# Mixing matrices in turn with the last unit's other side work, and three loads on GpSimd eight steps ahead

## The chip, the cores and the metric

The kernel runs on one core of one Trainium2 chip. The metric is the device time of one execution in microseconds (us), the median of three runs. A matmul runs on TensorE (PE; PEld is its load of weights), elementwise work on VectorE (DVE), exponentials and casts on ScalarE (ACT). GpSimd (POOL) and SyncE (SP) mostly issue DMAs. Each engine executes its own list of instructions in order; an engine that issues a DMA waits at that point until the semaphores for the transfer are met.

## The reference

The input `x` is (2, 128, 64, 64): two images, 128 channels, 4096 positions each.

```python
# layer 0
xn  = group_norm(x, 32 groups)
q, k, v = conv1x1(xn);  q, k = rotary2d(q), rotary2d(k)      # 4 heads of 32 channels
x   = xn + conv1x1(softmax(q k^T / sqrt(32)) v)
# layer 1, on tokens t (2, 4096, 128)
t = t + softmax(u u^T) u                    with u = layer_norm(t)
t = t + sum_i w_i * stu_i(layer_norm(t)[:, :4096 / 2**i])    # i = 0..3
w = one_hot(argmax(s)) - s + s,             s = softmax(log_weights + gumbel)
# stu(u): causal FFT convolution of u with 16 filters phi, then for each filter k
#   U_plus_k  @ M_phi_plus[i, k] * sigma_k**0.25 + U_minus_k @ M_phi_minus[i, k] * sigma_k**0.25
#   + three taps: sum_n shift(u, n) @ M_u[i, n]
```

The four branches differ only in their matrices and in where the input is cut off. So the kernel first forms one set of weighted matrices: for each filter k one plus and one minus matrix summed over the four branches (the "mixing matrices"), three tap matrices (`mu`), and a mask over the ends. That work reads only parameters and has no place of its own: it is side work, put beside the attention.

## The kernel before

The kernel has a main path in half precision (`in_halves`), which the profile shows, and a fallback that is not executed here.

*Layer 0* (`layer0`) runs four units (image b, two heads each). A unit has 16 rounds: two heads times eight chunks i of 512 queries. A round goes through 32 key tiles in 11 groups m: TensorE makes the scores of up to three key tiles (L209, called from the loop), ScalarE takes the exponential (L465), and TensorE weighs the values with it two groups later. The sum of a round lies in one PSUM accumulator `acc` with a single buffer. At the round's end `close` copies it to `accs` on VectorE (L413), and the next round's first weighing waits for that copy. Every second round `divide` (VectorE L366, L370, L371, L377, and small SP transfers) divides by the softmax sums and `project` multiplies with the output weights.

Side work is a Python generator: the loop calls `next(beside)` at certain groups of each round, and each call emits the instructions up to the next `yield`. Groups in `BESIDE` do so in the first three units, groups in `BESIDE_LAST` in the last one; other groups, in `DONE`, take a step of `divide` and `project`. In the last unit the side work is `beside_last`, 71 steps in 80 slots, one kind after another:

- nine steps of layer-norm statistics, then 17 steps of `normalise(0)`, which normalises the first image's tokens, transposes them on TensorE and splits them into the halves `hiT`, `loT`;
- `filters16`, 12 steps: loads of `phi` and `turned`, the branch weights, the 64 coefficients `coef`, eight table matmuls, and the writing of the tables to memory;
- `matrices16`, 33 steps through `combined`: for each of 16 filters, two 256 KB loads into one of two raw buffers in the tile `room` (L918, L919 on the queue `aside`, which is GpSimd), a weighted sum over the branches on VectorE (L750, L752), a sum and a difference (L929, L930), a store `mx[k]` (L931, GpSimd), and a maximum (L933).

The order of one engine's list is not always the order in the program. A scheduler places the instructions by its own estimates, except those marked `keep_in_program_order`, which include the products of layer 0 and the normalising steps. Tiles with the same `tag` share buffers and so wait for each other.

*Layer 1's attention* (`attend16`), image 0 first, goes over 36 pairs (j, i), i at least j, of blocks of 512 tokens. For a pair: `scores` makes y in two halves (L1185, three matmuls a tile), exponential on ScalarE (L1194), cast into the first part of `pair` (ScalarE, L1198), the remainder into its second part (VectorE, L1199). `turn` transposes both parts by DMA on SP (L1204) into `eT` if i > j. One pair later `direct` weighs tokens with `pair` (`od`, L1213) and adds into `oT` (L1225, L1227); two pairs later `across` adds up `eT` (`both`, L1232) and weighs with it (`oa`, L1213). `close` ends a row j.

This attention also takes side work: `chain(left, stats.steps(), rest16(p), normalise(1, ...))`, where `left` is what is left of layer 0's last division, `stats` are the second image's statistics, and `rest16` has two steps. The first, `mask_of`, loads `ends` (256 KB, L1025, GpSimd) and forms `mask`. The second, `means`, loads `mu_raw` (768 KB, L1030, ScalarE) and `gw` (128 KB, L1032, GpSimd; the matrix of the inverse transform) and forms `mu` and `gw`. Each load is emitted directly ahead of its use.

Somewhat before that GpSimd issues `fw` (L975, the matrix of the forward transform). SP also carries the first loads for the feed-forward part: two 1 MB loads `tables_a` (`chunk16`, L1483), which have buffers of their own and are placed early by the scheduler, between the transposes of `turn`.

After attention of both images come the transform of the tokens (`feed`), the convolution and mixing (L1541 to L1564), and the inverse transform (`back`).

Of the kernel before, what the change touches and what calls it, by code (L numbers as in the profile page):

```python
# [29 lines left out]
HALF = L // 2  # L30
GT = 3
BESIDE, DONE = (1, 5, 9), (2, 4, 7, 8)
BESIDE_LAST = (1, 3, 5, 6, 9)
NJ = HALF // P
NG = 32
NK = 16
# [40 lines left out]
def conv_attn_hybrid(ctx: ExitStack, tc: tile.TileContext, io):  # L77
# [680 lines left out]
    def layers(st, layer0, in_halves):  # L758
# [25 lines left out]
        def normalise(b, stats, stage, gate=None):  # L784


            for i in range(NQ):
                while gate is not None and gate[0] <= i:
                    yield
                cols = bass.ts(i, 512)  # L790
                y = stage(i, 0)
                for t in range(4):
                    stats.normed(y[:, bass.ts(t, P)], 4 * i + t)
                nc.vector.tensor_copy(hi[0][:, cols], y)
                yield
                pt = side[0](f"yT{b}_{i}")
                for t in range(4):
                    nc.tensor.transpose(pt[:, bass.ts(t, P)], y[:, bass.ts(t, P)], ident)
                nc.vector.tensor_copy(hiT[0][:, cols], pt)
                staged = b == 0 and not in_halves  # L800
                low = (stage(i, 1), stage(i, 0)) if staged else (loT[0][:, cols], lo[0][:, cols])
                for n, (src, first) in enumerate(((pt, hiT[0][:, cols]), (y, hi[0][:, cols]))):
                    nc.vector.tensor_tensor(low[n], src, first, ALU.subtract)
                    if staged:
                        nc.sync.dma_start(lows[i, n], low[n])
                yield
            if in_halves:
                nc.vector.reduce_max(spread[:, 2 * NK + b : 2 * NK + b + 1], stats.rs, axis=AX.X)
                yield

        def filters16(spare):

            phi = spare.tile([P, 2, TROW], F32, tag="tab", name="phi16")
            aside.dma_start(phi, io["phi"])
# [15 lines left out]
                nc.vector.tensor_copy(kept, x)  # L830
                chosen.append(kept)
            chosen.append(coefficients(new, wbr, M_SCALE))
            yield
            both = spare.tile([P, 2, L], F16, tag="ks", name="spectra")
            for s in range(2):
                tb = both[:, s, : 4 * 2 * TROW].rearrange("w (h i x) -> w h i x", h=2, i=2)
# [112 lines left out]
        def beside_last(stage, spare=None):  # L949
            first_parts()  # L950
            stages = [stage(n) for n in range(1 if in_halves else 2)]
            stats = LayerStats(last, tok[0], "a0")
            yield from stats.steps()
            yield from normalise(0, stats, lambda i, n: stages[n][:, i])
            if in_halves:
                yield from filters16(spare)
                yield from matrices16(spare)


        left = layer0(tok, px, last, side, beside_last)  # L960
# [67 lines left out]
        def means(p, wbr):  # L1028
            mu_raw = p.tile([P, NBR, NU, C], F32, tag="raw", name="mu_raw")
            nc.scalar.dma_start(mu_raw, io["mu"].rearrange("i n d e -> d i n e"))  # L1030
            weighted_sum(mu, mu_raw, wbr)
            aside.dma_start(gw, io["gw16" if in_halves else "gw"])  # L1032
            if in_halves:
                nc.vector.scalar_tensor_tensor(
                    gw, gw, OUT_SCALE, mask.unsqueeze(1).to_broadcast([P, 2, P]), ALU.mult, ALU.mult
                )
            else:
                nc.vector.tensor_tensor(gw, gw, mask.unsqueeze(1).to_broadcast([P, 2, P]), ALU.mult)

        def rest16(p):  # L1040
            wbr, top = chosen[:2]
            mask_of(p, top)
            yield
            means(p, wbr)
            yield

        def matrices(p):
# [334 lines left out]
        with ExitStack() as l1:  # L1382
# [3 lines left out]
            with ExitStack() as part:  # L1386
                p = pool(part, "l1_a")
                gate = [0]

                def second_parts(n):  # L1390
                    if n < NQ and not in_halves:
                        low = p.tile([P, 2, 512], F32, tag="low", name=f"low{n}")
                        nc.sync.dma_start(low, lows[n].rearrange("n p c -> p n c"))
                        copy = nc.vector.tensor_copy(loT[0][:, bass.ts(n, 512)], low[:, 0])
                        if n == 0:
                            tc.keep_in_program_order(copy)
                        nc.vector.tensor_copy(lo[0][:, bass.ts(n, 512)], low[:, 1])

                def ready(i):
                    second_parts(i + 1)  # L1400

                second_parts(0)
                fw = transform(p1)

                def closed(j):
                    gate[0] = j + 1

                y = [None]

                def stage(i, n):  # L1410
                    y[0] = p.tile([P, 512], F32, tag="y", name=f"y1_{i}")
                    return y[0]

                stats = LayerStats(p1, tok[1], "a1")
                own = (rest16(p),) if in_halves else (filters(p, fw), matrices(p))
                steps = chain(left, stats.steps(), *own, normalise(1, stats, stage, gate))
                (attend16(0, p1, steps, closed) if in_halves else attend(0, p1, steps, closed, ready))
            right0.close()
            if in_halves:
# [443 lines left out]
```

## Time and profile before

| | |
|---|---|
| median of three runs | 2777.88 us (2777.81 to 2810.39) |
| the profiled execution | 2786.72 us |
| its span, first to last instruction | 2784.9 us |
| mean granted TensorE clock | 0.977 |
| HBM read, written | 212.53 MB, 23.33 MB |
| layer 0's last unit, from the copy L413 at 787.87 to the one at 1045.06 | 257.2 us |

The page of the profile gives each engine's busy time, then the span in 40 equal slices of 69.6 us in which each digit is a busy share in tenths, then the DMA queues, the chain of work that ended last, and the costliest groups of instructions. Times are us from the start of the span. A line such as "L1213 ... <- DVE pair L1199: 13.4, 2, 6.7" says that L1213 waited for L1199's `pair` on VectorE: in total, how often, the longest. The lists of single instructions give start, duration, engine, line, and in brackets the idle time before it and what ended that. PEclk is the clock that the throttle granted TensorE.

Busy time by stretch around the change, for all of the region that the change touches (columns: stretch, length, busy time and instructions of PE, PEld, DVE, ACT, POOL, then clock, DMA share, GB/s):

```profile
786.00:871.00 85.00, 78.06 (x369) 41.06 (x368) 74.86 (x241) 78.05 (x61) 24.14 (x32) 1.00 0.22 66
871.00:956.00 85.00, 75.67 (x325) 37.12 (x324) 30.73 (x63) 71.29 (x54) 37.17 (x51) 0.96 0.54 96
956.00:1045.00 89.00, 88.30 (x423) 47.75 (x423) 24.07 (x40) 85.76 (x65) 0.56 (x1) 1.00 0.02 7
1045.00:1160.00 115.00, 84.14 (x356) 37.02 (x355) 76.65 (x209) 50.84 (x107) 17.57 (x20) 0.85 0.71 123
```

The first three rows are the last unit of layer 0: VectorE is nearly full in the first, and nearly all of the GpSimd and DMA work lies in the first two. The last row is the start of the second layer's attention.

### The profile page before, as it was taken

To read this page: it belongs to the slowest core of one execution; us is meant where nothing else is said; L and a number is where in the kernel's file an instruction comes from. 1 tells how busy PE (TensorE), PEld (TensorE's weight loads), DVE (VectorE), ACT (ScalarE), POOL (GpSimd) and SP (SyncE) were. 2 spreads that over 40 slices of the span, in tenths; PEclk is the share of its full clock that TensorE was granted. 3 is DMA by queue.
4 is the path that set the end of the run, shared out by engine and by line. 5 is a ranking of instruction groups with operands and counts; after the bars stand their busy time and mean duration, and the time that the engine had idled before them with its cause. 6 is when DMAs were issued, how large, how long until landed. Compare 5 with 4: busy or idle time off the path is not lost.

```text
span 2784.9 us, 32561 instructions
## 1 busy us (share of the span) xinstructions
PE 2588.1 (93%) x11955; PEld 1276.1 (46%) x11955; DVE 1668.5 (60%) x2946; ACT 1841.3 (66%) x2059; POOL 432.5 (16%) x711
## 2 busy tenths in 40 slices
PE   5999999999998996999989988898789999999998
PEld 3555555555544452444434443343344445445444
DVE  5256564246267225767886567575456666666664
ACT  4999999999998894556644555454345555555553
POOL 2022121012124201100043100111111111111110
PEclk9999999999999997999999998999999999999999
DMA  4122220012014307655375654666666666655662
GB/s 144 35 65 67 65 65 20 7 50 74 22 39 94 67 5 135 115 107 105 69 144 110 126 96 91 154 174 156 149 167 165 200 192 181 179 206 179 185 188 87
DMA packets 351051, 311.92 MB, mean 112 GB/s; under 512 B 292816, under 2 KB 303200, under 8 KB 334432
## 3 DMA queue, kind: packets, MB, share of 16 engines
q1 hardware_dynamic: 295376, 231.71, 32.6%
q0 software_dynamic: 52512, 74.81, 11.2%
q10 hardware_dynamic: 2992, 3.22, 0.4%
q8 instruction: 96, 1.57, 0.2%
q14 instruction: 75, 0.61, 0.1%
HBM read 212.53 MB, written 23.33 MB: 85 GB/s over the span
## 4 chain that ended last, share of the span: by engine, by line
PE 30%; DMA 13%; DVE 7%; issue 1%; ACT 1%; POOL 0%; SPq 0%; DVEq 0%; ACTq 0%; POOLq 0%
PE m L1557 19%; PE cv L1541 6%; DMA eT<-pair 5%; DMA tables_b<-tables 3%; DVE pair L1199 3%; DMA base<-oc 2%; DVE both L1232 2%; PE ar L1312 1%; DMA had<-base 1%; DVE x L1549 1%; PE bk L1669 1%; DMA tables_a<-tables 1%; DMA rows<-uh 1%; PE od L1213 1%; PE pf L1328 0%
## 5 line engine op out<-in xcount | busy, mean ns | idle before, releaser
L465 ACT ACTIVATE e<-s 128x1536 f16<-128x1536 f32 (+1 forms) x704 | 938.4, 1427 | 52.9 <-PE s L209 48.3
L1549 DVE TENSOR_TENSOR x<-cv,x 128x1024 f16<-128x1024 f32 x512 | 602.3, 1219 | 302.9 <-ACT x L1548 302.9
L1548 ACT CAST x<-cv 128x1024 f16<-128x1024 f32 x512 | 493.7, 1017 | 404.4 <-PE cv L1541 389.5
L1557 PE MATMUL m<-x,mxr 128*128 128x512 f16 x2048 | 622.5, 381 | 0.0
L209 PE MATMUL acc<-e,v 128*97 128x512 f16 x2048 | 559.0, 380 | 16.4 <-DVE accs L413 13.7
L209 PE MATMUL s<-qs,ks 128*128 128x512 f16 x2048 | 559.7, 380 | 7.9 <-ACT e L465 4.3
L1557 PE MATMUL m<-x,mxl 128*128 128x512 f16 x1024 | 391.4, 382 | 3.3 <-DVE oh L1564 3.2
L209 PEld LDWEIGHTS <-v 128*97 128x97 bf16 x2048 | 255.4, 125 | 229.8 <-issue 28.9
L1194 ACT ACTIVATE ey<-y,nshift 128x512 f32<-128x512 f32 x288 | 196.0, 685 | 225.3 <-PE y L1185 135.9
L1557 PEld LDWEIGHTS <-mxr 128*128 128x128 f16 x2048 | 201.3, 98 | 242.8 <-issue 5.3
L209 PEld LDWEIGHTS <-ks 128*128 128x128 f16 x2048 | 201.0, 99 | 229.6 <-issue 46.8
L1478 POOL DMA_DIRECT2D tokens<-rows x252 | 152.9, 611 | 845.5 <-PE cv L1541 819.8
L1232 DVE SCALAR_TENSOR_TENSOR both<-eT 128x512 f16<-128x512 f16 x224 | 153.6, 686 | 135.2 <-DMA eT<-pair 124.5
L1213 PE MATMUL od<-pair,hi 128*128 128x512 f16 x576 | 189.6, 391 | 30.0 <-DVE oT L1225 15.1
L1185 PE MATMUL y<-bothT 128*128 128x512 f16 x864 | 206.5, 381 | 4.0 <-ACT ey L1194 3.0
L1199 DVE TENSOR_TENSOR pair<-ey,pair 128x1024 f16<-128x1024 f32 x144 | 175.4, 1218 | 16.0 <-ACT pair L1198 15.6
L413 DVE COPY accs<-acc 97x512 f32<-97x512 f32 x64 | 44.1, 689 | 227.3 <-PE acc L209 227.1
L1541 PEld LDWEIGHTS <-tokens 128*128 128x128 f16 x1024 | 100.6, 99 | 164.5 <-issue 68.1
L1213 PEld LDWEIGHTS <-hi 128*128 128x128 f16 x1024 | 102.6, 100 | 146.2 <-issue 35.1
L1198 ACT CAST pair<-ey 128x1024 f16<-128x1024 f32 x144 | 150.2, 1043 | 24.6 <-DMA eT<-pair 11.4
L1557 PEld LDWEIGHTS <-mxl 128*128 128x128 f16 x1024 | 101.0, 99 | 131.6 <-DVE oh L1564 10.0
L1213 PE MATMUL oa<-eT,hi 128*128 128x512 f16 x448 | 146.6, 389 | 14.3 <-DMA eT<-pair 14.3
(221 smaller groups left out, 2297.5 us busy)
## 6 DMA issues: line engine op xcount, KB each, us to landing
tables_a<-tables SPq DMA_DIRECT2D x64, 1024.0 KB
tables_b<-tables SPq DMA_DIRECT2D x64, 1024.0 KB
tokens<-rows POOLq DMA_DIRECT2D x252, 128.0 KB, 12.2
tab<-in_rot SPq DMA_DIRECT2D x32, 512.0 KB
ks<-term POOLq DMA_DIRECT2D x112, 64.0 KB, 2.2
qs<-term POOLq DMA_DIRECT2D x112, 64.0 KB, 2.1
accs<-back SPq DMA_DIRECT2D x32, 128.0 KB
room<-in_mpp POOLq DMA_DIRECT2D x16, 256.0 KB, 3.4
```

Source lines behind the costliest of these rows:

```text
L209: tc.keep_in_program_order(nc.tensor.matmul(*args, **kw))
L465: nc.scalar.activation(e[:, own, :], ps[:, own, :], AF.Exp, scale=SCORE_SCALE)
L1185: nc.tensor.matmul(ps[:, q, :], a[0][:, bass.ts(t, P)], c[0][:, bass.ts(i, 512)], start=(n == 0), stop=(n == 2),)
L1194: nc.scalar.activation(e[:, q, :], ps[:, q, :], AF.Exp, bias=nshift16, accum_out=den[:, t, i : i + 1])
L1199: nc.vector.tensor_tensor(pair[:, 1, own], e, pair[:, 0, own], ALU.subtract)
L1213: nc.tensor.matmul(acc, a[0][:, own], pair(m, t), start=(start and t == 0 and n == 0), stop=(stop and t == 3 and n == 2),)
L1232: nc.vector.scalar_tensor_tensor(both, eT[:, 0, :, u, :], 1.0, eT[:, 1, :, u, :], ALU.mult, ALU.add, accum_out=den[:, 4 * i + u, j : j + 1],)
L1478: (nc.gpsimd if n else nc.sync).dma_start(ut[64 * copy : 64 * copy + 64], rows16[b].rearrange("h c r w d -> (h c) r w d")[:, row : row + B ...
L1541: ordered(nc.tensor.matmul(pu[:, h, :], ut[:, at, :], tt[:, :, at, :], start=True, stop=True))
L1548: nc.scalar.copy(hi, pur)
L1549: nc.vector.tensor_tensor(lo, pur, hi, ALU.subtract)
L1557: nc.tensor.matmul(acc, m, x, start=(s == 0 and i == 0), stop=(s == 1 and i == len(products) - 1))
```

## The change

Two things are changed. In the last unit of layer 0 the mixing matrices no longer follow the tables and the normalising: after the statistics, each slot takes a step of `normalise` and `filters16` and of `matrices16` in turn (`by_turns`). For this, loads, branch weights and coefficients of `filters16` move ahead of both into `branches16`, and `BESIDE_LAST` has six slots in a round, not five.

At the start of the second layer's attention, `rest16` issues the loads of `ends`, `mu_raw` and `gw` at its beginning, all three on GpSimd and into tiles without a shared tag. Then come the statistics' eight steps, and only then `mask`, `mu` and `gw` are formed, one step each.

```diff
-BESIDE_LAST = (1, 3, 5, 6, 9)
+BESIDE_LAST = (0, 1, 3, 5, 6, 9)
...
-        def filters16(spare):
+        def by_turns(*parts):
+            parts = list(parts)
+            while parts:
+                for part in list(parts):
+                    if next(part, parts) is parts:
+                        parts.remove(part)
+                    else:
+                        yield
+
+        def branches16(spare):
 
             phi = spare.tile([P, 2, TROW], F32, tag="tab", name="phi16")
             aside.dma_start(phi, io["phi"])
...
             chosen.append(coefficients(new, wbr, M_SCALE))
-            yield
+            chosen.append((phi, turned, most))
+
+        def filters16(spare):
+            phi, turned, most = chosen[3]
             both = spare.tile([P, 2, L], F16, tag="ks", name="spectra")
...
             yield from stats.steps()
-            yield from normalise(0, stats, lambda i, n: stages[n][:, i])
+            normed = normalise(0, stats, lambda i, n: stages[n][:, i])
             if in_halves:
-                yield from filters16(spare)
-                yield from matrices16(spare)
+                branches16(spare)
+                yield from by_turns(chain(normed, filters16(spare)), matrices16(spare))
+            else:
+                yield from normed
...
-        def rest16(p):
+        def rest16(p, steps):
             wbr, top = chosen[:2]
-            mask_of(p, top)
+            ends = p.tile([P, NBR, P], F32, name="ends")
+            aside.dma_start(ends, io["ends"].partition_broadcast(P))
+            mu_raw = p.tile([P, NBR, NU, C], F32, name="mu_raw")
+            aside.dma_start(mu_raw, io["mu"].rearrange("i n d e -> d i n e"))
+            aside.dma_start(gw, io["gw16"])
+            yield from steps
+            weighted_sum(mask, ends, top)
             yield
-            means(p, wbr)
+            weighted_sum(mu, mu_raw, wbr)
+            yield
+            nc.vector.scalar_tensor_tensor(
+                gw, gw, OUT_SCALE, mask.unsqueeze(1).to_broadcast([P, 2, P]), ALU.mult, ALU.mult
+            )
             yield
...
-                own = (rest16(p),) if in_halves else (filters(p, fw), matrices(p))
-                steps = chain(left, stats.steps(), *own, normalise(1, stats, stage, gate))
+                second = normalise(1, stats, stage, gate)
+                if in_halves:
+                    steps = chain(left, rest16(p, stats.steps()), second)
+                else:
+                    steps = chain(left, stats.steps(), filters(p, fw), matrices(p), second)
```

The remaining lines of the diff touch `means` for the fallback only.

More of the change, by code (lines that the diff above doesn't have):

```diff
@@ L1031, in means @@
             weighted_sum(mu, mu_raw, wbr)
[L1032 to L1038, printed above, removed]
-        def rest16(p):
-            wbr, top = chosen[:2]
-            mask_of(p, top)
-            yield
-            means(p, wbr)
+            nc.sync.dma_start(gw, io["gw"])
+            nc.vector.tensor_tensor(gw, gw, mask.unsqueeze(1).to_broadcast([P, 2, P]), ALU.mult)
+        def rest16(p, steps):
+            wbr, top = chosen[:2]
+            ends = p.tile([P, NBR, P], F32, name="ends")
[5 more added lines that the diff above has]
+            weighted_sum(mask, ends, top)
+            yield
+            weighted_sum(mu, mu_raw, wbr)
[3 more added lines that the diff above has]
+            )
             yield
```

## The prediction

> **What bounds the kernel now.** I read the page first, then busy time by stretches of 50 and 10 us, then the waits of the stretches in which TensorE falls short, last the order of single instructions there.
>
> ```profile
> span 2784.9 us, 32561 instructions
> PE 2588.1 (93%) x11955; PEld 1276.1 (46%) x11955; DVE 1668.5 (60%) x2946; ACT 1841.3 (66%) x2059; POOL 432.5 (16%) x711
> PE   5999999999998996999989988898789999999998
> ...
> PEclk9999999999999997999999998999999999999999
> ```
>
> TensorE is the bound: 2588 of 2785 us. Only its gaps, and stretches at a low granted clock, can be won. A slice is 69.6 us. Two dents lie near the change: slice 13 (835 to 905 us, inside the last unit of layer 0) and slice 16 (1044 to 1114 us, the start of the second layer's attention, where the clock row has its only 7 of this half). Cut finer:
>
> ```profile
> 1045.80:1072.30 26.50, 11.14 (x37) 3.97 (x37) 14.34 (x29) 8.68 (x20) 6.23 (x10) 0.72 0.38 114
> 1072.30:1098.40 26.10, 26.10 (x124) 12.81 (x123) 22.88 (x61) 16.65 (x34) 2.94 (x2) 0.96 1.07 139
> 1098.40:1115.70 17.30, 6.59 (x17) 2.28 (x16) 5.51 (x29) 3.65 (x8) 2.01 (x2) 0.61 0.80 154
> ```
>
> Columns: stretch, length, busy time and instructions of PE, PEld, DVE, ACT, POOL, then clock, DMA share, GB/s. In the middle row PE fires 124 instructions in 26.1 us, about 0.21 us each: full rate. The first row has 37 (8.0 us of work in 26.5), the third 17 (3.7 us in 17.3). So 18.5 and 13.6 us are lost. The waits of PE from 1045 to 1160 name the causes:
>
> ```profile
> PE od L1213 <- DVE pair L1199: 13.4, 2, 6.7
> PE oa L1213 <- DMA eT<-pair: 13.4, 4, 9.2
> ```
>
> Who holds `pair`? The order of VectorE, ScalarE and GpSimd in the first stretch:
>
> ```profile
> 1050.71 0.35 DVE L750 TENSOR_SCALAR room<-room,small 128x256 f32<-128x256 f32 x1 [2.87 <-DMA room<-in_mpm]
> ...
> 1055.68 0.35 DVE L750 TENSOR_SCALAR room<-room,small 128x256 f32<-128x256 f32 x1 [2.08 <-DMA room<-in_mpm]
> ...
> 1058.49 1.21 DVE L1199 TENSOR_TENSOR pair<-ey,pair 128x1024 f16<-128x1024 f32 x1
> ...
> 1067.23 0.29 DVE L750 TENSOR_SCALAR mask<-ends,top 128x128 f32<-128x128 f32 x1 [6.28 <-DMA ends<-in_ends]
> ...
> 1060.56 0.39 ACTq L1030 DMA_DIRECT2D mu_raw<-in_mu  x1
> 1060.99 1.05 ACT L1198 CAST pair<-ey 128x1024 f16<-128x1024 f32 x1 [9.92 <-DVE ao L366]
> ...
> 1043.17 0.56 POOL L931 DMA_DIRECT2D mx<-room  x1 [110.27 <-DVE room L930]
> ```
>
> The last four mixing matrices stand at the very end of the unit in VectorE's order and behind it, two of them wait there for their loads, and the first `pair` comes at 1058.5. The load of the means was put into ScalarE's order ahead of a cast of `pair` and holds it until 1060.6. Then VectorE waits 6.28 us for `ends`, issued only at 1060.97, with the second half of `pair` behind it (1069.4). GpSimd stood 110 us in the store of a matrix that VectorE had not finished.
>
> **What the Trainium skill says.** "DMA: Bandwidth & Descriptors", Anatomy of one DMA: DMA engines don't wait on semaphores; the wait is on the issuing sequencer before dispatch. The trace agrees: the issue of `mu_raw` kept ScalarE idle 9.92 us. The same page, Issuing engines are not separate DMA queues: transfers of all issuers end on the same 16 engines. So putting the load on GpSimd frees ScalarE's order and gives no bandwidth. "TensorE: Matmul & The Clock Gate", What's actually happening: a TensorE that idles falls to half clock and needs some us of work to recover. Here matmuls follow at 0.43 us instead of 0.216 after the waits (1110 to 1115 us), with 0.61 granted: agrees, so a removed stall gives back more than its own length.
>
> **The change part by part.** The order of instructions of both kernels, as built, is known: on every engine it is the same again from about pair (1,2) of the first attention on. So only 786 to 1155 us can differ, and what is won or lost there shifts everything after it.
>
> *Last unit, side work.* Steps: 9 statistics, 17 normalising, 12 tables, 33 matrices, 71 of 80 slots before; now 70 of 96 (one yield gone, six slots a round), the matrices alternating with the rest. Nothing is added to TensorE (32 transposes, 8 table matmuls as before). In VectorE's order all 16 matrices now lie ahead of the copy of the eighth accumulator; before, 12 did and 4 came last. VectorE's work between one accumulator copy (L413) and the next is, by the durations of the trace (weighted sum 1.9 us, two differences 0.57, maximum 0.41, a normalised chunk about 3.6, a divide 4.0), before 12, 18, 16, 15, 17, 12, 12, 1 us and after 14, 16, 16, 12, 16, 11, 14, 9. The copies were 14.5 us apart undisturbed and 14.5, 16.1, 16.5, 18.4, 16.5, 18.7, 19.4, 17.0 measured. The work is the same and slightly evener. Waits come on top: a buffer is refilled 2.5 us after the store's issue, two load issues take 1.5, landing 3.3 more, and the next matrix some 2.9 of VectorE, so about 10.3 us for two matrices in two buffers, at most 2.9 in 15 us. One round of the new order has four, so I expect a wait of about 4.5 us there, and 1 to 2.5 us in three or four others; before it was 9.6 us in four waits. Against that, the scattered table writes (32 issues of 0.75 us) now come after all matrices, so no load queues behind them, but they still meet the divide's transfers: those cost PE 4.5 and 1.7 us before (waits at 908 and 941), and one of the two should stay. Sum: 0, from -7 to +9.
>
> *Start of the attention.* Removed from between the last copy and the second `pair` half: the four matrices with waits, the held issue on ScalarE, the wait for `ends`. What is then late: y of (0,0) begins at 1045.8 as before, first cast done at 1050.4 as before, `pair` half one on VectorE to 1051.6, L366 to 1052.9 (1.22 each), second cast by 1052.2, half two to 1054.1; od of (0,0) ends near 1055.5, and the point that lay at 1072.4 comes at about 1056.4. Gain 16. The loads of `ends`, means and inverse matrix (256, 768, 128 KB) are issued behind `fw`, which waits for TensorE, so at about 1045 on GpSimd in some 2.5 us; nothing urgent is behind them (the next there are eight small powers). At the 200 to 350 GB/s that the same loads reached at 1060 to 1066 they are gone by about 1053, hidden by the ramp; if they hold back the small divide transfers, 2 us are lost, since the divide's product stands ahead of a `pair`. Their first use stands some 40 places later in VectorE's order than before: no wait. The nine small operations on them (mask, means, inverse; 0.3 to 0.6 us each) move in between later ones, hidden by TensorE's 7.8 us a pair (36 matmuls at 0.216). ACT loses one issue of 0.39 us. Gain 16, from 12 to 18.
>
> *An effect on SP's order.* Before, both 1 MB loads of `tables_a` are issued together at 1084.3, ahead of the transposes of pair (0,3), which land at 1110: the 9.2 and 1.5 us waits and the slow clock of the third row, 13.6 us. In the new order one load stands before the transposes of (0,3) and the other before those of (0,4). The two transposes of a pair take 4.3 us (the usual piece of the chain of waits); 1084.3 to 1110 is 25.7 us with some 2.5 pairs of them (10.8), so the two loads cost about 15, one 7.5. A pair's transposes are ready about 11.4 us before they are needed and take 4.3: 7 us of slack. 12 us of delay beyond it gave the stall of 9 to 10. With the loads apart, the first delays by some 4.7 (no stall), the second by about 8.7: a stall of 1.7 and a little slow clock. Gain 9; bounds 0 (the loads still pile up) and 13.
>
> Sum on the profiled execution: 2786.7 (span 2784.9 and 1.8 around it) - 16 - 9 + 0 = 2761.7. It stands 8.8 above the median of 2777.9, where the same 25 us give 2753.
>
> **The rivals.**
> - *Front only:* the `tables_a` loads cost the same wherever they stand, since the same 2 MB pass the same engines. For it: DMA share 1.07 and 0.80 around there. Against: slack of 7 us for each pair. Gain 16: 2762.
> - *Slower:* the matrix loads become the pace of layer 0's last unit. All 16 matrices are now squeezed between accumulator copies, an accumulator has one buffer, and each load that lands late holds the copy behind it and TensorE behind that. It decides when the rounds carry on average 3.1 us more wait than now over eight rounds (25 us); with 5 us it is +40 - 25, 2793. For it: the round with four matrices, and 4.1 us from issue to landing. Against: two buffers, and rounds of 10 to 12 us of work that leave room.
> - *No effect:* the ramp at 1046 is held by something that I took for done (the divide's transfers, or the loads at 1045), and the new waits take the 16 us back: 2778.
>
> **How the numbers follow.** Both gains 0.55, front only 0.25, no effect 0.10, slower 0.10. Predicted 2753. The likeliest's own bounds are 2777.9 less 38 and less 3 in the extreme; its middle part 2740 to 2764. The range reaches to front only and toward no effect: 2739 to 2772. A measurement of this kernel tells about 2% (55 us) from no change; the whole lost time in the touched stretches is 18.5 + 13.6 + 25 in the unit (257 us from copy to copy, against 16 times 14.5), so faster by 2% would need nearly all of it: 0.03. Slower by over 2% needs 10 us more in each of eight rounds: 0.03.
>
> **What would show it.** Right: no wait of `od` for `pair` over 2 us and no idle ScalarE near the start; PE over 20 us busy in the 26 after y of (0,0), against 11.1; `oa` waiting under 4 us in all for `eT`; the last unit 257 us within 8. Wrong: PE waits for `accs` well over 13.5 us, VectorE waiting for `room` over 25 us in the unit, or the 9 us wait for `eT` still there.

## The result and the profile after

| | before | changed |
|---|---|---|
| median | 2788.08 us (20 runs, 2771.60 to 2814.15) | 2769.99 us (20 runs, 2749.75 to 2791.76) |
| ratio | | 0.9940, 95% interval 0.9918 to 0.9963 |
| span of the profiled execution | 2784.9 us | 2769.4 us |

The ratio is 16.7 us of 2788, with an interval from 10.3 to 22.9; it leaves out runs that took over 1.5% more than the fastest run of the same kernel, so it differs a little from the ratio of the medians. A gain of 25 was forecast. The median of before was 2777.88 when three runs were known and is 10 higher with 20, so the absolute 2753 was also set on a low level.

From the page of the changed kernel, the busy times and the rows of TensorE and of its clock:

```profile
PE 2588.8 (93%) x11955; PEld 1276.7 (46%) x11955; DVE 1670.4 (60%) x2946; ACT 1841.7 (67%) x2059; POOL 434.3 (16%) x712
...
PE   5999999999998898999989997998779999999998
...
PEclk9999999999999999999999998999999999999999
```

Busy times are the same as before, so no work went away. In slice 16 TensorE's digit is 8 where it was 6, and the 7 in the clock row is gone; slices 13 and 14, in the last unit, are both 8 now. Busy time by stretch says it more closely (columns as before: stretch, length, PE, PEld, DVE, ACT, POOL, clock, DMA share, GB/s). The first row begins at the first score matmul of the attention, as the 26.5 us row of before did; the second is the stretch with the 1 MB loads; the last three are the last unit.

```profile
1050.10:1076.60 26.50, 25.30 (x122) 12.25 (x122) 20.43 (x36) 19.80 (x41) 0.00 (x0) 1.00 0.72 102
1082.80:1097.80 15.00, 10.49 (x33) 3.85 (x32) 9.68 (x44) 4.88 (x10) 2.16 (x3) 0.78 1.10 153
786.00:871.00 85.00, 76.90 (x349) 39.39 (x347) 69.70 (x223) 76.21 (x60) 26.21 (x35) 0.96 0.25 74
871.00:956.00 85.00, 78.09 (x338) 39.15 (x338) 46.32 (x101) 71.94 (x55) 36.31 (x51) 0.96 0.48 91
956.00:1049.00 93.00, 89.74 (x423) 47.95 (x422) 20.20 (x29) 85.47 (x65) 5.63 (x9) 0.98 0.17 36
```

TensorE is busy 25.3 of the first 26.5 us of the attention, where it was 11.1, and the clock is 1.00. The last unit needs 93 us for the 423 matmuls after 956, where before it needed 89. TensorE's waits in the same 115 us of attention as before:

```profile
PE oa L1232 <- DMA eT<-pair: 3.6, 3, 1.7
PE od L1232 <- DVE oT L1246: 2.6, 2, 2.2
...
PE od L1232 <- DVE pair L1218: 0.2, 1, 0.2
```

The two waits of 13.4 us for `pair` and for `eT` have become 0.2 and 3.6, and a new one for `oT` is 2.6. (Line numbers after the change are about 20 higher.)

From here on two lengths tell the kernels apart better than the whole time does. Each is read from one trace of a kernel. The *unit* is the time from the first to the last accumulator copy of layer 0's last unit (787.87 to 1045.06 before). The *start* runs from that last copy to the 41st `pair` subtraction. Behind that point all kernels below have the same order of instructions, and this rest alone took from 1526 to 1566 us in 14 profiles. A *round* is the time from one accumulator copy to the next; the unit has 16.

| kernel | unit | start | sum against before | ratio of times (95%) |
|---|---|---|---|---|
| before | 257.2 | 198.9 | | |
| changed | 263.1 | 172.9 | -20.1 | 0.9940 (0.9918 to 0.9963) |
| changed_again | 259.2 | 171.3 | -25.6 | 0.9884 (0.9832 to 0.9936) |
| mu_on_gpsimd | 260.9 | 181.9 | -13.3 | 0.9946 (0.9919 to 0.9973) |
| early_loads | 255.5 | 182.8 | -17.8 | 0.9964 (0.9938 to 0.9989) |
| turns_only | 265.8 | 177.7 | -12.6 | 0.9944 (0.9915 to 0.9974) |
| five_slots | 271.9 | 173.6 | -10.6 | 0.9948 (0.9918 to 0.9978) |
| three_buffers | 262.6 | 171.7 | -21.8 | 0.9912 (0.9884 to 0.9940) |
| later_tables | 264.4 | 172.4 | -19.3 | 0.9961 (0.9938 to 0.9985) |
| both_mended | 266.1 | 172.1 | -17.9 | 0.9935 (0.9908 to 0.9962) |
| six_slots_no_turns | 245.1 | 217.6 | +6.7 | 0.9991 (0.9963 to 1.0019) |
| even_matrices | 265.9 | 177.7 | -12.5 | 0.9947 (0.9922 to 0.9971) |
| even_loads_together | 262.9 | 175.7 | -17.4 | 0.9925 (0.9895 to 0.9956) |
| even_clear | 246.8 | 177.9 | -31.4 | 0.9869 (0.9821 to 0.9917) |

Most of the ratios overlap. The starts tell more: those of before, of the runs with one half of the change and of the whole change lie apart (198.9; 177.7 to 182.8; 171.3 to 173.6 for the changed kernel and its variants with matrices in turn). Units repeat less well, as the traces of one order below show.

### The profile page after: what moved, and what is told of

Its sections match the earlier page's. It is cut to its first block, busy times and chain, and to the rows that moved or that the text cites. A ratio compares the mean times of both kernels' runs of the same rounds, so it can differ in the third digit from the quotient of the medians.

```text
span 2769.4 us, 32569 instructions
## 1 busy us (share of the span) xinstructions
PE 2588.8 (93%) x11955; PEld 1276.7 (46%) x11955; DVE 1670.4 (60%) x2946; ACT 1841.7 (67%) x2059; POOL 434.3 (16%) x712
## 4 chain that ended last, share of the span: by engine, by line
PE 52%; DMA 24%; DVE 14%; ACT 6%; issue 3%; POOL 1%; SPq 0%; DVEq 0%; ACTq 0%; POOLq 0%
PE m L1579 17%; PE acc L209 11%; PE s L209 11%; DMA eT<-pair 8%; PE cv L1563 5%; ACT e L465 5%; DMA tables_b<-tables 4%; DVE pair L1218 4%; DMA tables_a<-tables 3%; DVE both L1251 3%; DMA rows<-uh 2%; DMA base<-oc 2%; DMA had<-base 1%; PE bk L1691 1%; PE od L1232 1%
## 5 line engine op out<-in xcount | busy, mean ns | idle before, releaser
L209 PE MATMUL acc<-e,v 128*97 128x512 f16 x2048 | 560.7, 381 | 17.1 <-DVE accs L413 14.5
L1563 PEld LDWEIGHTS <-tokens 128*128 128x128 f16 x1024 | 100.1, 99 | 163.4 <-issue 65.7
L1232 PEld LDWEIGHTS <-hi 128*128 128x128 f16 x1024 | 102.0, 100 | 130.8 <-issue 19.3
L1563 PE MATMUL cv<-tables_b,tokens 128*128 128x512 f16 x512 | 135.0, 387 | 23.2 <-DMA tables_b<-tables 22.6
## 6 DMA issues: line engine op xcount, KB each, us to landing
tokens<-rows POOLq DMA_DIRECT2D x252, 128.0 KB, 12.6
```

Source lines behind the costliest of these rows:

```text
L209: tc.keep_in_program_order(nc.tensor.matmul(*args, **kw))
L1232: nc.tensor.matmul(acc, a[0][:, own], pair(m, t), start=(start and t == 0 and n == 0), stop=(stop and t == 3 and n == 2),)
L1563: ordered(nc.tensor.matmul(pu[:, h, :], ut[:, at, :], tt[:, :, at, :], start=True, stop=True))
```

## The experiments

### The start: which part of the change brings it

**mu_on_gpsimd**, the kernel before with one word changed:

```diff
-            nc.scalar.dma_start(mu_raw, io["mu"].rearrange("i n d e -> d i n e"))
+            nc.gpsimd.dma_start(mu_raw, io["mu"].rearrange("i n d e -> d i n e"))
```

> The kernel before with one word changed: the load of the means is issued by GpSimd in place of ScalarE; matrices and the place of all loads in the program stay. As built, this alone puts both halves of the first pairs ahead of the mask in VectorE's order and one tables_a load on either side of the transposes of pair (0,3). Theory A (the start is late for three reasons that add: four matrices at the end of the unit, the held cast with the mask behind it, two 1 MB loads together): the unit stays at 257 us, the first pair half still comes 13 us after the last accumulator copy, the second 2.6 us behind it where it was 11; that gives about 8, the separated loads another 9, so 17 us less than before. Rival B (the loads cost the same wherever they stand): 8 us less, with a wait of 9 us for eT still there. Rival C (the start is held by the matrices alone): no more than 3 us less.

Measured: the start is 17.0 us shorter, as theory A said. VectorE's list at the start of this run:

```profile
1061.28 0.42 DVE L933 TENSOR_REDUCE spread<-room 128x1 f32<-128x256 f32 x1
1061.61 1.21 DVE L1199 TENSOR_TENSOR pair<-ey,pair 128x1024 f16<-128x1024 f32 x1
...
1064.18 1.23 DVE L1199 TENSOR_TENSOR pair<-ey,pair 128x1024 f16<-128x1024 f32 x1
```

The first half of `pair` still stands directly behind the last matrix, 13.6 us after the copy at 1048.05, and the second follows 2.6 us later, where it was 11. TensorE waits for `pair` once, 6.9 us, and no 9 us wait for `eT` is left (2.8 the longest). The unit took 260.9 with the order of before (257.2).

**early_loads**, the second half of the change alone: `rest16` as in the changed kernel, the matrices as before.

> Only the second half of the change: the loads of ends, means and inverse matrix on GpSimd at the head of the attention's side work, the matrices as before, one kind after the other. The order of VectorE around the start and that of SP are those of the run with the one word changed. Theory A: within 3 us of that run, so about 17 us less than before, unit 257 us: it is the issue's engine that matters, not the eight steps. Rival (the distance matters too, because ends and means land too late): 5 us or more less than the one-word run.

Measured: start 182.8, 0.9 from the one-word run. The engine of the issue brings the gain. What distance is worth stays open: VectorE and SP have the same order in both runs, and in both `ends` was issued 16 to 17 us after the last copy (at 1059.21 here), behind the store of the last matrix on GpSimd. So the eight steps changed neither the issue nor the order of use here.

**turns_only**, the first half alone: `by_turns`, `branches16` and six slots, with `rest16` as before.

> Only the first half of the change: matrices in turn with normalising and tables, six slots a round; mask, means and inverse matrix as before, with the means on ScalarE. As built, both tables_a loads stay together ahead of the transposes of pair (0,3). Theory A: the unit takes 263 us as in the changed kernel, 6 more than before; the first pair half comes some 6 to 9 us earlier after the last copy, the wait for eT of 9 us stays; together 0 to 6 us less than before. Rival (the longer unit of the changed kernel was chance): unit 257, 6 to 12 us less.

Measured: the unit is 265.8, 8.6 above before, and theory A holds there. In the start it holds for one part, and the sum, 12.6 us below before, lies outside its 0 to 6. Two of TensorE's waits in this run:

```profile
PE oa L1227 <- DMA eT<-pair: 11.1, 2, 9.5
PE od L1227 <- DVE pair L1213: 0.9, 2, 0.4
```

The 9.5 us wait for `eT` stays, because both `tables_a` loads still stand together. But the start is 21 us shorter. The issue of `mu_raw` on ScalarE came at 1051.06, before the last accumulator copy, and held no cast. (The profile of before puts that issue's wait down to VectorE's L366, but here L366 of the last divide starts only at 1060.28; what the issue really waited for is not shown.) With the matrices gone from the end of the unit, the cast is free even with `mu_raw` on ScalarE. So the held cast was a consequence of the four matrices too, and the two halves of the change do not add: 17 (or 16) and 21 apart, 26 and 27.6 together.

### The unit: why it became longer

Three profiles with the order of before gave 257.2, 260.9 and 255.5, mean 257.9. Three with the matrices in turn gave 263.1, 265.8 and 259.2, mean 262.7. So one order spreads by 5 to 7 us, and the two groups overlap: by the totals alone the 4.8 us would be weak evidence. The last is the changed kernel once more, run beside the last arrangements:

> The changed kernel itself once more, for a second trace and for times beside the next two. Theory A (two rounds of the last unit are longer by construction, 19.8 and 19.3 us): unit 262 to 266 us, the start 172 to 174 us from the last copy to the 41st half of a pair; everything behind differs from run to run by some 20 us. Rival (the long rounds of the first trace were chance): unit 257 to 259.

Its unit, 259.2, lies between the two expectations, but its rounds have the same two long ones, 19.9 and 17.8 us, where the first trace has 19.8 and 19.3. The rounds of all six traces say more than the totals (us):

| order, three traces each | third round | eleventh round | rounds 1 to 8 together | rounds 9 to 16 together |
|---|---|---|---|---|
| as before | 16.2 to 16.5 | 14.8 | 135.5 to 137.0, mean 136.4 | 120.0 to 124.2, mean 121.5 |
| matrices in turn | 19.8 to 21.4 | 17.8 to 20.4 | 135.5 to 138.8, mean 137.0 | 123.7 to 127.0, mean 125.6 |

The third and the eleventh are longer in every trace. But the fourth, sixth and seventh became shorter by about as much as the third became longer, so that the first eight rounds, which hold all the matrices, cost the same as before. The 4.8 us lie almost wholly behind them, in the eleventh.

The third round in the changed kernel's trace, VectorE's list at its end:

```profile
831.56 0.34 DVE L750 TENSOR_SCALAR room<-room,small 128x256 f32<-128x256 f32 x1
831.94 0.48 DVE L752 SCALAR_TENSOR_TENSOR room<-room,small 128x256 f32<-128x256 f32 x1
836.03 0.35 DVE L750 TENSOR_SCALAR room<-room,small 128x256 f32<-128x256 f32 x1 [3.61 <-DMA room<-in_mpm]
836.30 0.68 DVE L413 COPY accs<-acc 97x512 f32<-97x512 f32 x1
```

VectorE has no other gap in this round. Just ahead of the accumulator copy stands the first operation of the next matrix, which waits 3.6 us for its load; TensorE waited 4.8 us for that copy. Over the unit VectorE waits 20.2 us for loads in nine places, 9.6 in four before.

The eleventh is the round from 954.93 to 974.20. The tables are written to memory in two bursts of 16 small writes, one for each half. GpSimd's and VectorE's lists:

```profile
952.41 5.98 POOL L872 DMA_DIRECT2D tables<-spectra  x8 [2.15 <-DMA tables<-tables]
...
963.83 0.52 POOL L877 DMA_DIRECT2D tables<-tables  x1 [5.44 <-DMA tables<-spectra]
964.35 0.59 POOL L989 DMA_DIRECT2D fw<-in_fw  x1
964.93 0.55 POOL L1052 DMA_DIRECT2D ends<-in_ends  x1
...
965.74 1.22 DVE L377 TENSOR_TENSOR ao<-ao,accs 32x1024 f32<-32x1024 f32 x1 [5.84 <-DMA accs<-back]
```

The same product in the kernel before, where the copy was at 955.33:

```profile
962.55 1.22 DVE L377 TENSOR_TENSOR ao<-ao,accs 32x1024 f32<-32x1024 f32 x1 [3.65 <-DMA accs<-back]
```

The second burst of table writes runs into a divide. The divide's last product (L377) comes 10.8 us after the copy at 954.93, where before it came 7.2 us after its copy and TensorE did not wait for it. This is the first divide of the last head: its projection `po` stands ahead of the next scores in TensorE's order. The delay came while the burst was under way: the reciprocal waited 1.4 us for its input, and from the issue of `back` to that of the next transfer it took 3.5 us (959.93 to 963.45), 1.3 before; the last transfer was as quick as before. TensorE waited 2.5 us, and matmuls then ran slowly (clock 0.84 from 964.5 to 975).

**five_slots** puts `BESIDE_LAST` back to `(1, 3, 5, 6, 9)` in the changed kernel.

> The changed kernel with five side slots in a round of the last unit, as before, in place of six: 70 steps in 80 slots. As built, no round has more than three matrices (the changed kernel has one with four), and the table matmuls come some two rounds later. Theory A (the unit is 6 us longer for a load wait in the round with four matrices, 3.4 us, and for table writes that meet a divide whose product TensorE waits for, 4.5 us): the unit takes 256 to 261 us, and the run is 2 to 7 us below the changed kernel, so 19 to 24 below before. Rival (the matrices in turn cost the unit 6 us in any arrangement): unit 263, same time as the changed kernel, 16 below before.

Measured: the unit is 271.9, nine *longer* than in the changed kernel, and both theories miss. The load waits did not go (20.6 us in all): the fourth round took 21.0 us, and TensorE waited 6.6 us for its copy. The bursts moved two rounds down and met two divides of the last head; their rounds, the eleventh and the thirteenth, took 19.4 and 21.4 us. The second of these:

```profile
994.50 5.22 POOL L872 DMA_DIRECT2D tables<-spectra  x7 [1.87 <-DMA tables<-tables]
...
998.38 0.34 DVE L371 RECIPROCAL rec<-rec 32x32 f32<-32x32 f32 x1 [2.41 <-DMA rec<-accs]
1005.77 1.22 DVE L377 TENSOR_TENSOR ao<-ao,accs 32x1024 f32<-32x1024 f32 x1 [7.04 <-DMA accs<-back]
```

**later_tables** delays the tables by empty steps (`for _ in range(2): yield` ahead of each half).

> The changed kernel with four empty steps ahead of the tables' halves (two ahead of the first, two more ahead of the second), so that the second burst of table writes is released by a matmul late in the 11th round, and starts some 12 us after the copy that begins a divide, not 11 us ahead of it. Theory A (a burst that meets a divide costs little where nothing waits, and 4.5 to 6 us where a projection stands behind the divide in TensorE's order): the 19.3 us round becomes 15, the wait of po under 1 us, the unit 258 to 260 us. Rival (the divide is late for another reason, or the burst only moves to the next divide): one round of 19 us or more stays, the unit 263 or more.

Measured: the eighth to eleventh rounds, 16.4, 17.4, 14.4 and 19.3 us in the changed kernel, became 14.4, 15.0, 15.0 and 15.6. That the eleventh is short again once the burst starts after its divide shows that the burst had made it long. But the thirteenth went from 15.0 to 25.0: the rival's second case. What met the divide at 981.91 was not the burst but what follows it on GpSimd:

```profile
984.97 0.52 POOL L881 DMA_DIRECT2D tables<-tables  x1 [4.95 <-DMA tables<-spectra]
985.48 0.59 POOL L993 DMA_DIRECT2D fw<-in_fw  x1
986.06 0.55 POOL L1056 DMA_DIRECT2D ends<-in_ends  x1
986.60 1.05 POOL L1058 DMA_DIRECT2D mu_raw<-in_mu  x1
987.64 0.55 POOL L1059 DMA_DIRECT2D gw<-in_gw  x1
...
997.08 1.22 DVE L377 TENSOR_TENSOR ao<-ao,accs 32x1024 f32<-32x1024 f32 x1 [11.60 <-DMA accs<-back]
```

A copy of 992 KB and loads of 256, 256, 768 and 128 KB were issued in 3.2 us, in the middle of the divide. Its 4 KB transfer `back` was issued at 985.50 and followed by the next at 991.29: 5.8 us where the kernel before had 2.1. So the early loads of the change belong to the traffic that can hurt.

**three_buffers** gives the matrices a third raw buffer.

> The changed kernel with three raw buffers for the matrices in place of two (the third takes the room of the sums, which move to the small tile). As built, the scheduler puts 1, 2, 4, 3, 4, 2 matrices into the rounds of the first half where the changed kernel has 1, 2, 3, 2, 3, 3, 2. Theory A (VectorE's waits for loads, 20 us in nine waits in the changed kernel, set the longer rounds): these waits fall under 8 us and the unit takes 258 to 260 us instead of 263 to 266. Rival (VectorE is full in these rounds, and the waits only fill what is left): the unit stays at 263 or more, with TensorE's waits for accs still 14 us or above.

Measured: VectorE's load waits fell from 20.2 to 8.8 us and the third round from 19.8 to 16.3. But two rounds then have four matrices, one of them rose to 20.9, and the unit stayed at 262.6. The rival holds: in the first seven rounds of the changed kernel VectorE's work and its waits for loads fill 114 of 120.5 us (95.6 and 18.5), and what a load wait gives back is taken by other work. TensorE's waits for `accs` add up to 15 us, as the rival said.

**both_mended** joins the two:

> The changed kernel with three raw buffers and with the second half of the tables later. If both theories hold, the unit takes 254 to 257 us, the start stays as in the changed kernel (173 us from the last copy to the 41st half of a pair, before: 199), and the run is 6 to 9 us below the changed kernel, 22 to 26 below before. If the matrices in turn cost the same in any arrangement, the unit stays at 263.

Measured: unit 266.1, with the long sixth round of one parent (20.7 us) and the long thirteenth of the other (24.7). Nothing was mended.

**six_slots_no_turns** has six slots and the early loads, with the matrices after the tables:

> The kernel before with the loads of the second half of the change and six slots in a round, but matrices still after the tables, not in turn. As built, ten of the 16 matrices stand in VectorE's order in the last round and behind it. Theory A (what stands at the unit's end in VectorE's order delays the first pairs, at about 5 us a matrix with two buffers): the middle of the unit is quick, the first pair half comes 35 to 50 us after the last copy instead of 13, and the run takes 10 to 30 us more than before. Rival (the engine is idle enough there to catch up): within 5 us of the run with only the early loads.

Measured: the unit took 245.1, the shortest of all, and the start 217.6. The first `pair` came 49 us after the last copy, as theory A said, and TensorE waited 40.0 us for it. The time of the whole is that of before, not 10 to 30 us more, since the short unit pays for most of the late start; the sum of the two stages is 24.6 us above that of early_loads, so the rival misses. In this run GpSimd's list shows where the matrices had been:

```profile
1012.48 0.56 POOL L931 DMA_DIRECT2D mx<-room  x1 [103.72 <-DVE room L930]
```

GpSimd stood 104 us in the store of a matrix that VectorE had not summed, though from 908 to 1008 VectorE was busy for 24.2 us of 100: the scheduler had put the sum behind later work in VectorE's list. The first eight rounds, here with two matrices in place of 12 or 16, take 122.5 us, 137.0 before and 136.8 in the changed kernel. That points at the matrices among the normalising, though the bursts of table writes meet other rounds here too.

### A version from these findings

**even_matrices** takes normalising and tables first, then the matrices at two a round in the second half, with their sums and what stands around them held to the program's order (`pinned` is `keep_in_program_order` under a condition; the first part is shown against the kernel before):

```diff
+                for _ in range(7):
+                    yield
-                yield from matrices16(spare)
+                for n, _ in enumerate(matrices16(spare)):
+                    yield
+                    if n % 2 == 0:
+                        yield
...
-                nc.vector.tensor_copy(accs[:, bass.ts(half, 512)], acc[: NV * CH + 1, :])
+                pinned(nc.vector.tensor_copy(accs[:, bass.ts(half, 512)], acc[: NV * CH + 1, :]), (b, h) == (B - 1, NH - 1))
```

> A new arrangement from what the runs showed: normalising and tables first, seven empty steps, then the matrices at two a round in the second half of the unit, where VectorE is idle for three quarters; their sums, the accumulator copies, the divides and the projections of the last head, mask and means are held to the program's order on VectorE, so that the scheduler can't gather the matrices at the end. The early loads of the change are kept; one tables_a load stands on either side of the transposes of pair (0,3). If the unit was long because matrices and normalising share the full rounds, the unit takes 245 to 250 us (six slots without turns: 245 without matrices in it), the start 172 to 176, so 30 to 38 us less than before and 12 to 20 less than the changed kernel. Rival (matrix loads of 10 us for two take the rounds of the second half, 14.7 us long): rounds of 16 to 18 us there, unit 260 or more.

Measured: the first eight rounds are 14.4 to 16.2 us, but three later ones 21.4 to 21.8, and the unit is 265.9. The rival's 260 or more came, but its rounds of 16 to 18 us did not. In each of the three, a matrix that stood between the divide's first sum and its second delayed the reciprocal: `back` was issued 6.5 us after the copy (942.17 to 948.70 in the first), against 3.6 for an undisturbed one (985.67 to 989.27 before). The divide's last product came 11.8 to 12.7 us after the copy; the rest of that delay lies in the transfers behind the reciprocal. TensorE's largest wait from there on:

```profile
PE po L212 <- DVE ao L381: 12.1, 3, 4.5
```

**even_loads_together** differs only in the place of the means' sums and with it of the `tables_a` loads:

> The even arrangement with the sums of the means not held to the program's order. As built, this puts one or two of them among the first pairs and both tables_a loads together ahead of the transposes of pair (0,3), and changes nothing else. It measures that term by itself: theory A (two loads together overrun the slack of a pair): a wait for eT of about 9 us, and the start 4 to 9 us longer than in the even arrangement; rival (the same 2 MB cost the same wherever they stand): within 1 us.

Measured: the wait for `eT` is there, 10.0 us in one piece, but the start is 2.0 us *shorter* than with the loads apart. Starts of nearly one order differ by as much (171.3 to 173.6), so the rival is nearer. With the loads apart, this arrangement waits 7.7 us for `oT` and 3.2 for `eT`.

**even_clear** moves the empty steps so that no matrix stands inside a divide: six ahead, and two after every four steps.

> The even arrangement with six empty steps in place of seven and two empty steps after every four of the matrices, so that no matrix stands in VectorE's order between the first and the second sum of a divide (in the even arrangement one did, and delayed the divide's transfers by 3.3 us, which three projections then waited for). If that was what made the rounds of 21 us, these become 15 to 16 and the unit takes 248 to 253 us, with the start at 171 to 178; then 26 to 34 us less than before, and less than the changed kernel. Rival (matrix loads meet the divide's transfers in every round): rounds of 18 us or more stay, the unit 259 or more.

Measured: no round is above 16.9 us, TensorE waits 1.8 us in all at `po`, the unit is 246.8. The ratio to before is 0.9869 (0.9821 to 0.9917), the median 2755.36. The sum of unit and start is 31.4 us below before, and 6 to 11 below the changed kernel's two traces; the ratios of those two overlap with this one. Busy time by stretch in this run:

```profile
786.00:871.00 85.00, 84.16 (x391) 43.77 (x389) 63.27 (x191) 80.87 (x63) 16.19 (x20) 1.00 0.13 22
871.00:956.00 85.00, 81.33 (x360) 40.28 (x358) 39.29 (x80) 79.97 (x62) 33.58 (x49) 0.98 0.51 104
956.00:1033.00 77.00, 74.95 (x363) 40.81 (x362) 37.00 (x81) 72.89 (x55) 17.97 (x27) 1.00 0.28 86
```

TensorE has 391 matmul instructions in the first 85 us, 349 in the changed kernel; VectorE's work in the last row is 37 us where it was 20. By halves of the unit, the first eight rounds, now without matrices, take 125.8 us in place of 136.8, and the last eight, which hold all 16, take 120.9, as before the change (120.0 to 124.2). This supports the reading that it counts which rounds hold the matrices, and where in a divide they stand. It rests on one trace of this arrangement; the 12 to 16 us against the changed kernel's two traces are more than the 5 to 7 by which units of one order spread.

## Why the prediction was right or wrong

*What bounds it, and where the dents are:* right as to places. As far as the stages show, the gain lies in the second dent, the start; the first, inside the last unit, got no better. One reading beside a quoted rule was off: 0.61 is the clock from 1098.4 to 1115.7 us; from 1110 to 1115 it is 0.50, which fits matmuls at twice the distance better still.

*Start of the attention, gain 16:* right, by all its signs. The two `pair` halves came 5.4 and 8.0 us after the last copy (13.4 and 24.4 before), the second 16.4 us sooner. `od` waits 0.2 us for `pair`, TensorE is busy 25.3 of 26.5 us. Less right was the picture of three causes that add: turns_only shows that the held issue on ScalarE went with the matrices.

*SP's order, gain 9:* the whole start is 26.0 and 27.6 us shorter in the two traces of the changed kernel, against 25 for both terms. Taken by itself the term was too large. From the second `pair` half to the end of the start, before takes 174.5 us; turns_only and even_loads_together, with the loads together, take 168.5 and 167.8; kernels with the loads apart take 163.4 to 166.1, save the two even ones with 169.8 and 169.9. So the separation is worth at most 2 to 5 us in the changed kernel's order (turns_only differs from it also in the place of mask and means) and nothing that shows in the even one. The other 6 us of before's 174.5 fall away without the separation; mask and means among the first pairs are a possible cause that no run isolated. That the two terms together came so near is in part luck. The expected stall of 1.7 us is there (1.7 the longest), with `oT` beside it.

*Last unit, 0 us:* this is the step that failed. By the means of three traces each the unit is 4.8 us longer, inside the stated bounds of -7 and +9. Of the two terms of its sum, one came out by offset and one was wrong:

- Waits for loads. "I expect a wait of about 4.5 us" in the round with four matrices: VectorE waited 4.7 us there, in three pieces, but TensorE only 0.9 for the copy, and the round took 17.1 us, 18.7 before. What cost time was the 3.6 us directly ahead of a copy in the third round, which holds three normalised chunks; that round is 4.1 us longer by the means. In all VectorE waited 20.2 us for loads, where the prediction's own list adds up to 14.5 at the most. The first eight rounds still take 137.0 us against 136.4, since other rounds became shorter. The prediction's nothing is met here, but not by its working: "the work is the same and slightly evener" was read from sums per round, which show neither these waits nor where they stand.
- Table writes. "One of the two should stay" of the waits behind them (4.5 and 1.7): this is where the 4.8 us come from. Both bursts still met a divide. The first met the one in the ninth round, on which no matmul waits, and cost TensorE 1.7 us at the next copy, the same as in that round before. The second met the first divide of the last head, whose product TensorE waits for in order: 2.5 us of waiting, and an eleventh round of 19.3 us (17.8 and 20.4 in the other two traces) in place of 14.8. The prediction counted how many divides the bursts would meet, not what stands behind each.

*Loads of ends, means and inverse matrix at about 1045:* wrong in place. GpSimd issued them from 964.93 on, the last done at 967.1, inside the unit, since `fw` ahead of them did not wait for TensorE there. In the changed kernel they come just behind the issue of the divide's last transfer (963.45); in later_tables they come in the middle of a divide.

*The sum:* the touched stages gained 20.1 and 25.6 us in two traces, by the means of the units and starts 258 + 199 less 263 + 172, so 22. The interval of the ratio, 10.3 to 22.9, holds 20 and 22, and the 25 of the forecast lies just outside. The second, smaller set of runs of the changed kernel (changed_again, 0.9884) gives 32 us, from 18 to 47, and holds 25. So the whole time does not settle by how much the sum was off; the stages put it at some 3 us too much. The absolute time missed by 17 us, of which 10 are the level of before.

*Rivals:* front only foresaw 16, nearest in number to the 16.7, but for another reason: its wait for `eT` is not there. No effect is out: the interval does not reach it. The slower rival named a mechanism that the third round shows (a late load holds the copy behind it), but over eight rounds 0.7 us are left of it, not 25. What was held against it, "rounds of 10 to 12 us of work", does not fit the prediction's own list, where five of eight rounds have 14 or more; with 15.9 us of work in the third round there was no room for a wait.

*Signs:* all the signs named for a right prediction came true, the unit within 8 us of 257 among them. They were too wide to catch the term that failed.

## What to carry to other kernels

When side work moves, list for each DMA burst what stands behind the transfer that it meets. In the changed kernel the last product of a division that only VectorE waits for came 16.1 us after its copy and cost TensorE 1.7 us; one behind which TensorE has its next matmul in order came after 10.8 us and cost 2.5 us of waiting, in a round that became 4.5 us longer. Sums of work per round are not enough where a wait can stand directly ahead of the operation that frees an accumulator; read the last two instructions ahead of that operation. And the scheduler's order can differ from the program's: an issuer that stands for 100 us in a store while the engine that it waits for is mostly idle (24 of 100 us busy here) is a sign to hold the order by hand.

## What the runs showed that was not expected

In a divide, a 4 KB transfer took 5.8 us from its issue to the next step's issue where 2.4 MB of other transfers were issued around it, and 2.1 us in the kernel before without them.

A stall of TensorE cost more than its length: the wait of 2.5 us for `po` came with a round 4.5 us longer, one of 7.1 us with a round 10 longer (15.0 to 25.0), with clocks of 0.84 and 0.75 granted in the stretches behind.

The same instructions behind the touched stages took 1526 to 1566 us from run to run, more spread than the whole change. Part of it lies in waits for the 1 MB loads of the convolution (`cv` for `tables_b`): 14.9 us in all in both_mended, whose rest took 1526 us, and 29.0 in mu_on_gpsimd, whose rest took 1561.

What starts it was not tried. Nor is it settled why the two even arrangements wait longer for `oT` in the start (7.7 and 7.2 us) than the changed kernel (2.6).
